# Last layer norm of a graph transformer block: which engine finishes which tile, and who issues the stores

## The chip, the core and the metric

The kernel runs on one core of a Trainium2 chip. The core has five engines with queues of their own: TensorE (PE, matrix products), VectorE (DVE), ScalarE (ACT), GpSimd (POOL) and SyncE (SP, which here only issues transfers). They wait for one another by semaphores. SBUF is the on-chip memory with 128 partitions; PSUM holds the results of TensorE in eight banks of 128 x 512 fp32. The metric is the device time of one execution in microseconds; the median of several runs counts.

## What is computed

The reference takes 1250 nodes with 512 features each and 41,250 edges. It normalizes `x`, sends it through a two-layer graph network and a linear attention, adds both to `x`, and then adds a feed-forward block whose weights are mixed from eight experts by a gate. Only the last lines matter here:

```python
h = jax.nn.relu(jnp.einsum('bsd,bfd->bsf', x, W1m) + b1m[:, None, :])
out = jnp.einsum('bsf,bdf->bsd', h, W2m) + b2m[:, None, :]
res = x + out
mu = res.mean(axis=-1, keepdims=True)
var = res.var(axis=-1, keepdims=True)
return (res - mu) * jax.lax.rsqrt(var + LN_EPS) * lng + lnb
...
x = x + _L0_ffn_ref(_layernorm(x, axis=-1)[None], ...)[0]
```

For each row: the second product (256 to 512), plus the normalized input, a mean and a variance over 512 columns, the difference scaled by `lng`, plus `lnb`, plus the row of `x`.

## The kernel before, in words

The 1250 rows are ten tiles of 128 rows (`NT` = 10, the last has 98). The whole kernel is one straight program of some 7,000 instructions: input norm, the adjacency matrix counted from the edge list, two graph layers as dense products with it, the attention, the middle norm, the gate, and the feed-forward block. From line 1200 on, the order of the work is written out by hand (`given()`, a manual schedule): each engine takes its instructions in the order in which the program names them, and a wait holds up all that is queued behind it on that engine.

The change touches the last stage. Before it, the merged weights `m1` and `m2` are done, `joined` (line 1325) has made the hidden layer `a_t`, and `xn2` (the normalized input) has had the second bias added, tiles 0 to 4 by VectorE and tiles 5 to 9 by GpSimd (lines 1364 and 1366). `x_sb` holds the row of `x` with `lnb` added already, `ln_g` holds the scale.

For a tile `t` the last stage has these steps:

- `out_product` (line 1374): TensorE makes the second product in a fresh PSUM bank; ten tiles use eight banks in turn.
- `out_sum` (line 1378): VectorE adds `xn2` in place, in PSUM.
- `out_gauge`: `spread` (lines 586 to 590) has VectorE take `bn_stats` and `bn_aggr` (mean and variance in `mv`) and ScalarE the square root of variance plus epsilon (`rs`).
- then one of two ways to finish. `out_far` (tiles 0, 1, 3, 4, 6, 7, 8): ScalarE negates the mean (1402), VectorE takes the reciprocal (1403), ScalarE multiplies the two (1404) and normalizes the tile from PSUM to a row buffer in SBUF (`normal`, line 600), and GpSimd multiplies by `ln_g` (1406) and adds `x_sb` (1407). `out_near` (tiles 2, 5, 9): VectorE does it alone with two `scalar_tensor_tensor` instructions and a reciprocal between them (1392 to 1394).
- a store of 256 KB to `out`, issued by SyncE; tile 9's (98 rows, 196 KB) by ScalarE.

The loop at line 1410 sets the order: at step `t`, the product and sum of tile `t`, then the finish of tile `t - 1`, then the statistics of tile `t`. On VectorE, then, the finish of a near tile stands between the sum and the statistics of the next tile. The row buffers come from two groups: even tiles take one of three (`row`), odd tiles one of four (`xt`), so tiles 6, 8 and 9 wait until the stores of tiles 0, 2 and 1 have landed. `small` gives four buffers each for `mv` and `rs`.

After the last step each engine loads one flag (line 1419) and branches over a general version of the kernel that these inputs don't need (line 1426).

Of the kernel before, what the change touches and what calls it, by code (L numbers as in the profile page):

```python
# [9 lines left out]
F32 = mybir.dt.float32  # L10
# [3 lines left out]
AF = mybir.ActivationFunctionType  # L14
ALU = mybir.AluOpType
AX = mybir.AxisListType

P = 128
N = 1250
D = 512  # L20
DT = D // P
NT = 10
# [22 lines left out]
def rows(t):  # L45
    return min(P, N - t * P)
# [479 lines left out]
def usual_block(  # L526
# [23 lines left out]
    nc = tc.nc  # L550
# [4 lines left out]
    small = ctx.enter_context(tc.tile_pool(name="small", bufs=4))  # L555
# [9 lines left out]
    def large(place, shape, dtype=F32, name="large"):  # L565

        return big.tile(shape, dtype, tag=place, name=name)
# [12 lines left out]
    eps = const.tile([P, 1], F32, name="eps")  # L580
    nc.vector.memset(eps, EPS)

    def spread(src, n):

        st = small.tile([P, 6], F32, name="st")
        nc.vector.bn_stats(st[:n], src)  # L586
        mv = small.tile([P, 2], F32, name="mv")
        nc.vector.bn_aggr(mv[:n], st[:n])
        rs = small.tile([P, 2], F32, name="rs")
        nc.scalar.activation(rs[:n, 0:1], mv[:n, 1:2], AF.Sqrt, bias=eps[:n])  # L590
        return mv, rs
# [7 lines left out]
    def normal(dst, src, rs, n):  # L599
        nc.scalar.activation(dst, src, AF.Identity, bias=rs[:n, 1:2], scale=rs[:n, 0:1])  # L600
# [85 lines left out]
    for t in range(NT):  # L686
        n = rows(t)
# [453 lines left out]
    ln_g = late.tile([P, D], F32, name="ln_g")  # L1141
# [29 lines left out]
    xn2 = large("A", [P, NT, D], name="xn2")  # L1171
# [92 lines left out]
    for t in range(NT):  # L1264
        n = rows(t)
# [95 lines left out]
    for t in range(NT):  # L1361
        n = rows(t)
# [5 lines left out]
    last = {}  # L1368

    def out_product(t):  # L1370
        n = rows(t)
        last[t] = bank()
        for f in range(FT):
            nc.tensor.matmul(last[t][:n], a_t[:, f, t * P:t * P + n], m2[:, f, :], start=(f == 0), stop=(f == FT - 1))  # L1374

    def out_sum(t):
        n = rows(t)
        nc.vector.tensor_tensor(last[t][:n], last[t][:n], xn2[0:n, t, :], ALU.add)

    def out_gauge(t):  # L1380
        last[t] = (last[t],) + spread(last[t][:rows(t)], rows(t))

    def out_row(t):
        tag, bufs = (("row", 3), ("xt", 4))[t % 2]
        return tmp.tile([P, D], F32, tag=tag, bufs=bufs, name="m")

    def out_near(t):

        n = rows(t)
        ps, mv, rs = last[t]  # L1390
        m = out_row(t)
        nc.vector.scalar_tensor_tensor(ps[:n], ps[:n], mv[:n, 0:1], ln_g[:n], op0=ALU.subtract, op1=ALU.mult)
        nc.vector.reciprocal(rs[:n, 0:1], rs[:n, 0:1])
        nc.vector.scalar_tensor_tensor(m[:n], ps[:n], rs[:n, 0:1], x_sb[0:n, t, :], op0=ALU.mult, op1=ALU.add)
        (nc.scalar if t == NT - 1 else nc.sync).dma_start(out=out[t * P:t * P + n, :], in_=m[:n])

    def out_far(t):

        n = rows(t)
        ps, mv, rs = last[t]  # L1400
        m = out_row(t)
        nc.scalar.mul(mv[:n, 0:1], mv[:n, 0:1], -1.0)
        nc.vector.reciprocal(rs[:n, 0:1], rs[:n, 0:1])
        nc.scalar.activation(rs[:n, 1:2], mv[:n, 0:1], AF.Copy, scale=rs[:n, 0:1])
        normal(m[:n], ps[:n], rs, n)
        nc.gpsimd.tensor_tensor(m[:n], m[:n], ln_g[:n], ALU.mult)  # L1406
        nc.gpsimd.tensor_tensor(m[:n], m[:n], x_sb[0:n, t, :], ALU.add)  # L1407
        nc.sync.dma_start(out=out[t * P:t * P + n, :], in_=m[:n])

    for t in range(NT + 1):  # L1410
        if t < NT:
            out_product(t)
            out_sum(t)
        if t >= 1:
            (out_near if t - 1 in (2, 5, 9) else out_far)(t - 1)
        if t < NT:
            out_gauge(t)
    last_order.close()
# [4 lines left out]
def graph_block(tc, *args):  # L1423

    unusual = usual_block(tc, *args)
    with tc.If(unusual > 0):
        general_block(tc, *args)
# [58 lines left out]
```

## Time and profile before

| | |
|---|---|
| three runs | 574.11, 574.61, 574.74 us, median 574.61 |
| the profiled execution | 574.88 us |
| its span, first to last instruction | 572.9 us |
| mean granted TensorE clock | 0.981 |
| busy: PE, DVE, ACT, POOL | 546.3, 324.8, 242.0, 80.1 us |
| last stage: first and last product | 541.42, 558.75 us |
| last compute instruction of VectorE | 563.15 to 563.90 us |
| last compute instruction of GpSimd | 565.97 to 567.23 us |
| last store issued by SyncE | 567.26 us |

The profile is of one execution. Positions such as 541.42 are microseconds from the first instruction. A row in the lists of groups gives the line, the engine, the instruction, what it writes and reads, how often it ran, its busy time in all and the mean length of one in nanoseconds. PE busy is not PE at its peak, since matmuls are pipelined. L600, L586, L588 and L590 are lines of helpers that several stages use. In the last stage alone, by the list of groups from 541 us on, one of each took:

| line | engine | what | ns |
|---|---|---|---|
| 1378 | DVE | sum, 128 x 512 in PSUM | 688 |
| 586 | DVE | statistics | 695 |
| 588 | DVE | aggregate | 182 |
| 1403 | DVE | reciprocal, one column | 157 |
| 600 | ACT | normalize, PSUM to SBUF | 777 |
| 590 | ACT | square root, one column | 286 |
| 1402 | ACT | negation, one column | 188 |
| 1404 | ACT | product, one column | 294 |

### The profile page before, as it was taken

How to read it: one execution, taken by the hardware profiler on the slowest of the kernel's cores; microseconds unless marked ns; L12 is line 12 of the kernel's file. 1: busy time of each engine (PE TensorE's matmuls, PEld its weight loads, DVE VectorE, ACT ScalarE, POOL GpSimd, SP SyncE). 2: the span in 40 equal slices, each digit the busy share in tenths (PEclk: the TensorE clock that was granted, in tenths of full speed). 3: DMA queues.
4: the chain of work that ended last, by engine and by line, in shares of the span. 5: the costliest groups of instructions: out<-in, count | busy, mean ns of one | idle time of the engine just before them, and what ended most of it. 6: DMA issues, size and time to landing. Idle time of an engine off the chain costs nothing.

```text
span 572.9 us, 6957 instructions
## 1 busy us (share of the span) xinstructions
PE 546.3 (95%) x2367; PEld 369.1 (64%) x2367; DVE 324.8 (57%) x1097; ACT 242.0 (42%) x533; POOL 80.1 (14%) x77
## 2 busy tenths in 40 slices
PE   8799999999999999999999999999999999997990
PEld 7665568799955477777854454459995557764540
DVE  4579999976899734444425534111113248708693
ACT  5676664454444112322333443113323456727242
POOL 7200000000000000000013331000000001106975
PEclk9899999999999999999999999999999999997995
DMA  9400200020030020000311002000009120402023
GB/s 287 176 1 1 74 2 1 1 74 2 1 113 36 0 74 0 1 1 1 111 37 52 22 1 73 0 0 1 2 0 348 55 74 1 146 1 75 0 76 110
DMA packets 19285, 29.10 MB, mean 51 GB/s; under 512 B 1529, under 2 KB 8185, under 8 KB 19240
## 3 DMA queue, kind: packets, MB, share of 16 engines
q1 hardware_dynamic: 18984, 28.32, 14.6%
q8 instruction: 20, 0.33, 0.2%
q10 hardware_dynamic: 256, 0.25, 0.2%
q14 instruction: 25, 0.20, 0.1%
HBM read 26.01 MB, written 2.56 MB: 50 GB/s over the span
## 4 chain that ended last, share of the span: by engine, by line
PE 87%; DVE 5%; ACT 3%; POOL 2%; issue 1%; DMA 1%; POOLq 0%; DVEq 0%; ACTq 0%
PE bank L576 28%; PE bank L981 16%; PE bank L968 12%; PE bank L917 6%; PE bank L1037 6%; PE bank L849 5%; PE bank L1064 5%; PE bank L1325 3%; PE bank L606 2%; PE bank L1374 1%; POOL m L1406 1%; POOL m L1407 1%; DVE st L586 1%; PE bank L902 1%; ACT xn L600 1%
## 5 line engine op out<-in xcount | busy, mean ns | idle before, releaser
L981 PE MATMUL bank<-adj,y_h 128*128 128x416 f32 (+1 forms) x240 | 86.5, 361 | 1.1 <-DVE adj L851 1.1
L981 PE MATMUL bank<-adj,y_l 128*128 128x416 f32 (+1 forms) x240 | 84.4, 352 | 0.0
L834 DVE TENSOR_SCALAR oh_k<-count,e_d 128x240 f16<-128x240 f16 x324 | 82.6, 274 | 0.0
L1083 POOL TENSOR_TENSOR m<-m,ls_bc 128x512 f32<-128x512 f32 (+1 forms) x10 | 12.7, 1269 | 447.3 <-ACT m L600 447.3
L968 PE MATMUL bank<-w,h_t 128*128 128x512 f32 (+1 forms) x160 | 70.4, 592 | 0.0
L576 PE MATMUL bank<-z_t,w 128*128 128x416 f32 (+1 forms) x192 | 68.9, 513 | 0.0
L576 PEld LDWEIGHTS bank<-z_t,w 128*128 128x128 f32 x192 | 36.1, 189 | 31.8 <-issue 29.9
L832 DVE TENSOR_SCALAR oh_s<-count,s_lo 128x128 f16<-128x128 f16 x220 | 54.1, 246 | 0.0
L968 PEld LDWEIGHTS bank<-w,h_t 128*128 128x128 f32 (+1 forms) x160 | 29.4, 188 | 34.8 <-issue 34.5
L614 DVE SCALAR_TENSOR_TENSOR z_t<-u,m_sb,z_t 128x416 f32<-128x416 f32 (+1 forms) x24 | 15.7, 653 | 59.8 <-ACT u L613 59.8
L981 PEld LDWEIGHTS bank<-adj,y_h 128*128 128x128 f32 x240 | 45.1, 188 | 2.6 <-issue 2.1
L981 PEld LDWEIGHTS bank<-adj,y_l 128*128 128x128 f32 x240 | 45.2, 188 | 1.2 <-issue 0.7
L849 PE MATMUL bank<-oh_k,oh_s 128*128 128x240 f16 x324 | 41.4, 266 | 1.4 <-ACT oh_s L818 1.2
L849 PEld LDWEIGHTS <-oh_s 128*128 128x128 f16 x324 | 31.6, 98 | 15.8 <-issue 5.1
L612 ACT ACTIVATE z_t<-bank,v_sb 128x416 f32<-128x416 f32 (+1 forms) x24 | 14.6, 608 | 61.5 <-PE bank L981 61.5
L851 DVE TENSOR_TENSOR adj<-adj,bank 128x240 f32 x81 | 32.3, 399 | 13.9 <-PE bank L849 12.5
L995 DVE BATCH_NORM_STATS2 bst<-bank 128x6 f32<-128x416 f32 (+1 forms) x24 | 14.4, 600 | 42.9 <-ACT h_t L994 42.9
L917 PE MATMUL bank<-kk,xn 128*128 128x128 f32 (+1 forms) x320 | 38.4, 275 | 0.0
L576 PE MATMUL bank<-xn_t,lw 128*128 128x256 f32 (+2 forms) x128 | 37.6, 439 | 0.3 <-ACT xn_t L607 0.3
L917 PEld LDWEIGHTS bank<-kk,xn 128*128 128x128 f32 (+1 forms) x320 | 37.0, 192 | 0.1
L1064 PE MATMUL bank<-mixer,q_t 128*128 128x512 f32 (+1 forms) x80 | 36.3, 592 | 0.0
L576 PE MATMUL bank<-xn_t,gw 128*128 128x256 f32 (+2 forms) x128 | 35.3, 427 | 0.9 <-ACT xn_t L607 0.9
(166 smaller groups left out, 800.0 us busy)
## 6 DMA issues: line engine op xcount, KB each, us to landing
t<-in_tv_w SPq DMA_DIRECT2D x12, 512.0 KB, 7.5
w<-in_conv_w SPq DMA_DIRECT2D x4, 1024.0 KB, 5.5
x_in<-in_x SPq DMA_DIRECT2D x9, 256.0 KB, 4.6
xt<-in_x SPq DMA_DIRECT2D x9, 256.0 KB, 4.1
out<-m SPq DMA_DIRECT2D x9, 256.0 KB, 2.4
rest<-in_tv_w SPq DMA_DIRECT2D x4, 512.0 KB, 4.8
lw<-in_lin_w SPq DMA_DIRECT2D x4, 256.0 KB, 4.9
wk<-in_w_qkv SPq DMA_DIRECT2D x1, 1024.0 KB, 7.0
```

What stands on the lines that cost most here:

```text
L576: nc.tensor.matmul(ps[:, :cn], lhs(c), rhs(c), start=(c == 0), stop=(c == k - 1))
L614: nc.vector.scalar_tensor_tensor(dst, u[:, :cn], minus(*slope), dst, op0=ALU.mult, op1=ALU.add)
L832: nc.vector.tensor_scalar(oh_s[:, j, :], count16[:, 0:P], s_lo[:, b, j:j + 1], None, op0=ALU.is_equal)
L834: nc.vector.tensor_scalar(oh_k[:, j, :], count16, key[:, b, j:j + 1], None, op0=ALU.is_equal)
L849: nc.tensor.matmul(ps[:, 0:NT * W], oh_s[:, j, :], oh_k[:, j, :], start=(j == 0), stop=(j == J - 1))
L851: nc.vector.tensor_tensor(adj_r[:, :, at], adj[:, :, at], ps[:, 0:NT * W].rearrange("p (s d) -> p s d", s=NT), ALU.add)
L917: nc.tensor.matmul(ps[:, c * P:(c + 1) * P], xn[0:n, t, c * P:(c + 1) * P], k_nodes(f)[0:n, t, :], start=(t == 0), stop=(t == NT - 1))
L968: nc.tensor.matmul(ps[:n], h_t[:, c, t * P:t * P + n], w1[:, c, :], start=(c == 0), stop=(c == DT - 1))
L981: nc.tensor.matmul(ps[:, :cn], y[0:n, s, f * P:(f + 1) * P], adj_r[0:n, s, c0:c0 + cn], start=(s == 0 and y is ys[0]), stop=(s == NT - 1 a ...
L1037: nc.tensor.matmul(ps[:n], xn_t[:, c, t * P:t * P + n], wq[:, c, :], start=(c == 0), stop=(c == DT - 1))
L1064: nc.tensor.matmul(ps[:n], q_t[:, h, t * P:t * P + n], mixer[:, h, :], start=(h == 0), stop=(h == DT - 1))
L1325: nc.tensor.matmul(ps[:, :cn], m1[:, c, f * P:(f + 1) * P], xn2_t[:, c, c0:c0 + cn], start=(c == 0), stop=(c == DT - 1))
```

## The change

Tiles 4, 5, 7, 8 and 9 are finished by VectorE (`NEAR`), tiles 0, 1, 2, 3 and 6 by ScalarE and GpSimd. For four of the near tiles, 5, 7, 8 and 9 (`BY_SCALAR`), the sum also gives the row's total (`accum_out`), and ScalarE makes the statistics: the negated mean, the square of each difference summed over the row (the squares themselves go to the row buffer and are written over later), and the square root. VectorE adds this negated mean where it subtracted the mean. These four tiles are finished three steps after their sum, at the head of a step, ahead of that step's sum; tile 4 is finished one step after its sum, also at the head. All ten stores are issued by SyncE.

```diff
+    NEAR, BY_SCALAR = (4, 5, 7, 8, 9), (5, 7, 8, 9)
+
     def out_sum(t):
         n = rows(t)
-        nc.vector.tensor_tensor(last[t][:n], last[t][:n], xn2[0:n, t, :], ALU.add)
+        ps = last[t]
+        if t in BY_SCALAR:
+            mv = small.tile([P, 2], F32, name="mv")
+            nc.vector.scalar_tensor_tensor(ps[:n], ps[:n], 1.0, xn2[0:n, t, :], op0=ALU.mult, op1=ALU.add,
+                                           accum_out=mv[:n, 0:1])
+            last[t] = ps, mv
+        else:
+            nc.vector.tensor_tensor(ps[:n], ps[:n], xn2[0:n, t, :], ALU.add)
 
     def out_gauge(t):
-        last[t] = (last[t],) + spread(last[t][:rows(t)], rows(t))
+        n = rows(t)
+        if t in BY_SCALAR:
+            ps, mv = last[t]
+            rs = small.tile([P, 2], F32, name="rs")
+            m = out_row(t)
+            nc.scalar.mul(mv[:n, 0:1], mv[:n, 0:1], -1.0 / D)
+            nc.scalar.activation(m[:n], ps[:n], AF.Square, bias=mv[:n, 0:1], accum_out=mv[:n, 1:2])
+            nc.scalar.activation(rs[:n, 0:1], mv[:n, 1:2], AF.Sqrt, bias=eps[:n], scale=1.0 / D)
+            last[t] = ps, mv, rs, m
+        else:
+            last[t] = (last[t],) + spread(last[t][:n], n) + (None,)
...
     def out_near(t):
         n = rows(t)
-        ps, mv, rs = last[t]
-        m = out_row(t)
-        nc.vector.scalar_tensor_tensor(ps[:n], ps[:n], mv[:n, 0:1], ln_g[:n], op0=ALU.subtract, op1=ALU.mult)
+        ps, mv, rs, m = last[t]
+        m = out_row(t) if m is None else m
+        nc.vector.scalar_tensor_tensor(ps[:n], ps[:n], mv[:n, 0:1], ln_g[:n],
+                                       op0=ALU.add if t in BY_SCALAR else ALU.subtract, op1=ALU.mult)
         nc.vector.reciprocal(rs[:n, 0:1], rs[:n, 0:1])
         nc.vector.scalar_tensor_tensor(m[:n], ps[:n], rs[:n, 0:1], x_sb[0:n, t, :], op0=ALU.mult, op1=ALU.add)
-        (nc.scalar if t == NT - 1 else nc.sync).dma_start(out=out[t * P:t * P + n, :], in_=m[:n])
+        nc.sync.dma_start(out=out[t * P:t * P + n, :], in_=m[:n])
...
-    for t in range(NT + 1):
+    for t in range(NT + 3):
+        for u in NEAR:
+            if u == t - (3 if u in BY_SCALAR else 1):
+                out_near(u)
         if t < NT:
             out_product(t)
             out_sum(t)
-        if t >= 1:
-            (out_near if t - 1 in (2, 5, 9) else out_far)(t - 1)
+        if 0 < t <= NT and t - 1 not in NEAR:
+            out_far(t - 1)
         if t < NT:
             out_gauge(t)
```

In the built program VectorE's order from tile 4 on is: sum 4, reciprocal 3, statistics and aggregate 4, finish 4, sum 5, sum 6, statistics and aggregate 6, sum 7, reciprocal 6, finish 5, sum 8, sum 9, finish 7, finish 8, finish 9. In the new file the far way's GpSimd passes are lines 1428 and 1429, the near finish lines 1413 to 1416, the accumulating sum line 1384, the plain sum line 1388, ScalarE's statistics lines 1397 to 1399, the stores lines 1417 and 1430, the flag line 1444.

More of the change, by code (lines that the diff above doesn't have):

```diff
@@ L1389, in out_near @@
         n = rows(t)
-        ps, mv, rs = last[t]
-        m = out_row(t)
-        nc.vector.scalar_tensor_tensor(ps[:n], ps[:n], mv[:n, 0:1], ln_g[:n], op0=ALU.subtract, op1=ALU.mult)
+        ps, mv, rs, m = last[t]
+        m = out_row(t) if m is None else m
+        nc.vector.scalar_tensor_tensor(ps[:n], ps[:n], mv[:n, 0:1], ln_g[:n],
+                                       op0=ALU.add if t in BY_SCALAR else ALU.subtract, op1=ALU.mult)
         nc.vector.reciprocal(rs[:n, 0:1], rs[:n, 0:1])
         nc.vector.scalar_tensor_tensor(m[:n], ps[:n], rs[:n, 0:1], x_sb[0:n, t, :], op0=ALU.mult, op1=ALU.add)
-        (nc.scalar if t == NT - 1 else nc.sync).dma_start(out=out[t * P:t * P + n, :], in_=m[:n])
+        nc.sync.dma_start(out=out[t * P:t * P + n, :], in_=m[:n])
     def out_far(t):
         n = rows(t)
-        ps, mv, rs = last[t]
+        ps, mv, rs, _ = last[t]
         m = out_row(t)
```

## The prediction

> **What bounds the kernel now.** I read the granted clock first (0.981 for the whole span), then the chain that ended last in its last 50 us, then busy time by stretch for the end, then the engines' timelines there. The profiled execution took 574.88 us for a span of 572.9. TensorE carries the chain until tile 2 of the last product. The chain's view of the final stretch (start, length, what) then ends on GpSimd:
>
> ```profile
> 541.59 6.88 PE bank L1374 x16
> ...
> 558.66 0.79 ACT m L600
> 559.52 1.27 POOL m L1406
> 560.86 1.26 POOL m L1407
> ...
> 566.43 0.80 POOL m L1407
> ```
>
> Two stretches of the view of busy time (length; then PE, PEld, DVE, ACT, POOL busy with counts; clock, DMA share, GB/s) show what runs while GpSimd finishes:
>
> ```profile
> 560.00:567.30 7.30, 0.00 (x0) 0.00 (x0) 3.70 (x9) 2.51 (x7) 7.00 (x6) 0.59 0.41 148
> 567.30:573.00 5.70, 0.00 (x0) 0.00 (x0) 0.00 (x0) 0.00 (x0) 0.00 (x0) 0.50 0.15 53
> ```
>
> TensorE is done at 558.75. GpSimd works 7.00 of the next 7.30 us, VectorE 3.70. Seven of ten tiles go through GpSimd at two passes of 1.264 us (rows of lines 1406 and 1407), 2.55 us a tile, while VectorE needs 1.55 us for its share of such a tile. The last store, tile 8's, is issued by SyncE at 567.26, when GpSimd stops. From there to the end of the span are 5.68 us without a compute instruction. In SyncE's own waits,
>
> ```profile
> SPq L1426 <- SPq L1426: 2.7, 1, 2.7
> ```
>
> is its branch after the last store: code that it waits for, not data. The store's data landed 2.06 us after its issue and is covered. So the end stands 5.68 us behind SyncE's last store, and the question is when that is issued after the change.
>
> **The units of the sum.** From the timeline (start, length, engine, line, instruction), VectorE only, then the end of tile 9:
>
> ```profile
> 554.52 0.68 DVE L1378 TENSOR_TENSOR bank<-bank,xn 128x512 f32<-128x512 f32 x1
> 555.11 0.75 DVE L1392 SCALAR_TENSOR_TENSOR bank<-bank,mv,ln_g 128x512 f32<-128x512 f32 x1
> 555.77 0.15 DVE L1393 RECIPROCAL rs<-rs 128x1 f32<-128x1 f32 x1
> 555.96 0.75 DVE L1394 SCALAR_TENSOR_TENSOR m<-bank,rs,x_sb 128x512 f32<-128x512 f32 x1
> 556.62 0.69 DVE L586 BATCH_NORM_STATS2 st<-bank 128x6 f32<-128x512 f32 x1
> 557.35 0.18 DVE L588 BATCH_NORM_AGGREGATE mv<-st 128x2 f32<-128x6 f32 x1
> 557.45 0.68 DVE L1378 TENSOR_TENSOR bank<-bank,xn 128x512 f32<-128x512 f32 x1
> 558.04 0.15 DVE L1403 RECIPROCAL rs<-rs 128x1 f32<-128x1 f32 x1
> 558.16 0.70 DVE L586 BATCH_NORM_STATS2 st<-bank 128x6 f32<-128x512 f32 x1
> ...
> 563.15 0.75 DVE L1394 SCALAR_TENSOR_TENSOR m<-bank,rs,x_sb 98x512 f32<-98x512 f32 x1
> 563.94 0.60 ACTq L1395 DMA_DIRECT2D out<-m  x1
> ```
>
> Neighbours overlap, so I count from start to start: sum to the next 0.59 (0.71 where statistics follow a sum at once); reciprocal to statistics 0.12; statistics to aggregate 0.73 to 0.74; aggregate to the next sum 0.10, but 0.21 where the next one needs its result (562.03 to 562.24 in tile 9). A near finish is 0.66 + 0.19 + 0.66 = 1.51. A store follows its finish by 0.04 (563.90 to 563.94).
>
> **Part 1, GpSimd loses tiles 4, 7 and 8, and keeps 0, 1, 2, 3 and 6.** Six passes go, 6 x 1.264 = 7.6 us. It starts at 547.16 as before. Its tile 3 is done four tiles of 2.58 us later, at 557.5. Tile 6 waits for ScalarE's normalization, at about 558.0 by the count below, so GpSimd stops near 560.6. It leaves the path; VectorE is late next.
>
> **Part 2, VectorE.** It gains two near finishes (five for three), drops four statistics and four aggregates, and its sum in tiles 5, 7, 8 and 9 becomes a scalar_tensor_tensor with an accumulated row sum. The trace has no such instruction. Without the accumulator its row is that of line 1392: 0.75 us, 0.66 to the next. For the accumulator I call the extra r. Here the Trainium skill speaks against the change: "VectorE: DVE Perf Modes", section "Two Vector instructions with no wait between them", says that an operation that also writes out its accumulator is two instructions, the main one and an accumulator read. The trace has it on ScalarE alone:
>
> ```profile
> L1198 ACT ACTIVATION_READ_ACCUMULATOR u<-bank,v_sb 128x1 f32 x16 | 3.1, 193 | 0.0
> ```
>
> I take r = 0.19 from this row, near VectorE's own one-column rows (0.15 reciprocal, 0.18 aggregate). Without a second instruction r is 0. At most I allow 0.35, the read plus the 0.09 of overlap and about 0.07 of start lost.
>
> Up to the sum of tile 3 at 548.49 nothing differs. Sums 0 to 3 stand at TensorE's pace, (548.49 - 543.34) / 3 = 1.72, so sum 4 starts at 550.21. Then, in the built program's order:
> - to sum 5: 0.59 (reciprocal 3), 0.12, 0.74, 0.21, and the near finish of tile 4, 1.51: 553.38.
> - to sum 6: 0.66 + r = 0.85: 554.23.
> - to sum 7: 0.71 + 0.73 + 0.10: 555.77.
> - to sum 8: 0.85, 0.12, near finish of tile 5, 1.51: 558.25.
> - to sum 9: 0.85: 559.10. TensorE has it ready at 550.21 + 5 x 1.72 = 558.81.
> - near finishes of 7, 8 and 9: first at 559.95, then 561.46 and 562.97. Tile 9's last instruction starts at 563.82 and ends at 564.57.
>
> The last store is issued at 564.61: **2.65 us before 567.26**. With r = 0 VectorE runs into TensorE at sum 9, and the gain is 3.1. With r = 0.35 it is 2.0.
>
> **Part 3, ScalarE.** Each scalar tile has a negation (0.19), the Square with its accumulator (0.78 by line 600's row, then a 0.19 read that overlaps it by 0.09), and a square root (0.28), with small gaps 1.33 us. Reciprocal 6, at 556.62, lets it normalize tile 6 at 557.21. Tiles 7, 8 and 9 follow: Squares read out at about 559.0, 560.3 and 561.7, where VectorE asks at 559.95, 561.46 and 562.97. Cover: 1.0 to 1.3 us. Beyond it, each us that ScalarE is late counts in full.
>
> A second rule speaks against this part: "ScalarE: Activation LUTs", section "What ACT_TABLE_LOAD costs", puts every switch to a different table set at about 2.66 us. The trace agrees: 1.283 for the row, 2.70 from the load at 66.90 to the next activation. If Square and Sqrt were in different sets, four tiles would make up to eight switches, over 21 us. The built program has a load at the same three places as before, none among these lines; I take nothing.
>
> **Part 4, stores.** Order on SyncE: tiles 0, 1, 2, 3, 4, 6, 5, 7, 8, 9. Tile 4 waits behind tile 3 (557.5) and tile 5 behind tile 6 (560.6); nobody reads either row buffer again. The stores of 7, 8 and 9 come 1.51 us apart, and an issue takes 0.33 to 0.38, once 1.20, so SyncE keeps up. A load of 98 rows took it 0.36. ScalarE's 0.60 issue goes. Row buffers of tiles 6, 8 and 9 wait for stores 0, 2 and 1, landed by about 557.5. All this is nothing; if the last issue takes 1.20, it costs 0.85.
>
> **Sum.** 574.88 - 2.65 = 572.2 against the profiled execution, which is 0.27 above the median. Against the median, 574.61 - 2.65: **572.0 us**.
>
> **Rivals.**
> - *The cover is thinner* (12%): ScalarE's steps wait on one another and take half as long again, 2.0 us a tile for 1.33: tile 9's read comes at 563.7, 0.7 late; with 0.3 of a longer tail behind the last store 1.0 is lost: 573.0. For it: the engines' code fetches come closer together. Against: two stores were in flight at the earlier fetches too.
> - *The accumulating sum runs at half rate* (9%): 512 elements more at VectorE's pace (the step from 256 to 512 elements, 0.489 to 0.756, gives 0.53), four times that is 2.1 us: gain about 0.5, 574.1, no change. Against: without an accumulator it runs at one pace from PSUM and SBUF (416 columns from SBUF took 0.653, on the line between those two). VectorE's turn-over is at r = 0.85.
> - *Square and Sqrt evict each other's table* (6%, with any other cause of slower): six switches after tile 6's normalization, 16.2 us, less 1.3 of cover, on top of 572.0: about 587. It turns slower from 4 us of ScalarE delay over three tiles (1.3 + 2.65). Against it stands the built program.
>
> **Numbers.** Forecast 73%, rivals 12, 9 and 6. About 0.2% (1.15 us) can be told from no change: faster 0.85, same 0.09, slower 0.06. The forecast's own range is 3.1 to 2.0 of gain with 0.3 of scatter: 571.2 to 572.9. Reaching over the first rival: 571.2 to 573.5.
>
> **What would show it.** Right: the chain ends on VectorE, line 1416 of the new kernel; TensorE's end unmoved; GpSimd idle after 560.6; SyncE's last issue near 564.6 with about 5.7 us behind it; an accumulator-read row of about 0.19 on VectorE. Wrong: a gap on VectorE before line 1413 put down to ScalarE (cover too thin), a long row for line 1384 (half rate), a table load among lines 1397 to 1399, or SyncE's last issue late though VectorE was not.

## The result and the profile after

The changed kernel takes **571.18 us** (median of six runs, 570.89 to 572.49), the kernel before beside it 574.39 (six runs, 573.93 to 575.25). The ratio is 0.9948, with a 95% interval from 0.9936 to 0.9959, or 2.4 to 3.7 us less. A second set of five runs gave 571.63 us and 0.9947 (0.9932 to 0.9961).

The profiled execution took 570.89 us, its span is 569.1 us, the mean granted clock 0.989. The span is 3.86 us shorter than before's, but 1.02 us of that lies ahead of the edit: the last product starts at 540.40 instead of 541.42. The second profile of the same changed kernel, at a clock of 0.984, starts it at 541.48. That microsecond comes and goes with the clock: over the thirteen profiles of this document the last product starts at 540.1 to 540.8 us where the clock was 0.986 or more, and at 541.3 to 541.6 us where it was 0.985 or less. So below I count from the start of the first last product: before, 25.84 us to SyncE's last store and 5.68 from there to the end of the span, 31.52 in all; after, 22.80 and 5.88, 28.68 in all. The gain is 2.8 us, made of 3.04 in the stage less 0.2 in the tail.

The chain that ended last, its last pieces (start, length, what), now lies on VectorE:

```profile
561.57 0.75 DVE bank L1413
562.32 0.07 DVE rs L1415
562.39 0.02 issue
562.42 0.75 DVE m L1416
```

Busy time for the two stretches from TensorE's end on, in the columns of the earlier view:

```profile
557.70:563.20 5.50, 0.03 (x1) 0.00 (x0) 5.14 (x11) 2.49 (x9) 1.53 (x2) 0.99 0.70 260
563.20:569.10 5.90, 0.00 (x0) 0.00 (x0) 0.00 (x0) 0.00 (x0) 0.00 (x0) 0.50 0.15 46
```

GpSimd is busy 1.53 us of this stretch, where it had 7.00 of 7.30. VectorE fills 5.14 of 5.50: it is the one that finishes. Behind it stands the same empty tail. SyncE's waits still name the branch:

```profile
SPq L1451 <- SPq L1451: 2.5, 1, 2.5
```

During that wait, from 564.7 to 567.1 us, the view of the DMA queues has three packets on an instruction queue (packets, MB, share of the DMA engines):

```profile
q14 instruction: 3, 0.02, 3.2%
```

That SyncE waits for code is read from these two lines. VectorE's own branch falls into the same stretch, so not every packet need be SyncE's.

VectorE's timeline (start, length, engine, line, instruction, with the idle time ahead of it in brackets) shows both the new instruction and what limits the end:

```profile
552.39 0.69 DVE L1384 SCALAR_TENSOR_TENSOR bank<-bank,xn 128x512 f32<-128x512 f32 x1
553.00 0.14 DVE L1384 DVE_READ_ACCUMULATOR bank<-bank,xn 128x1 f32 x1
553.00 0.73 DVE L1388 TENSOR_TENSOR bank<-bank,xn 128x512 f32<-128x512 f32 x1
...
557.38 0.14 DVE L1384 DVE_READ_ACCUMULATOR bank<-bank,xn 128x1 f32 x1
557.87 0.70 DVE L1384 SCALAR_TENSOR_TENSOR bank<-bank,xn 98x512 f32<-98x512 f32 x1 [0.34 <-ACT rs L1399]
558.48 0.14 DVE L1384 DVE_READ_ACCUMULATOR bank<-bank,xn 98x1 f32 x1
558.48 0.76 DVE L1413 SCALAR_TENSOR_TENSOR bank<-bank,mv,ln_g 128x512 f32<-128x512 f32 x1
```

The accumulator read is an instruction of its own, 0.14 us long, but the sum of tile 6 starts in the same hundredth of a microsecond, 0.61 after the accumulating sum. Ahead of sum 9 VectorE is idle. The view names ScalarE, whose square root in tile 7 ended at 557.86. But sum 9 does not read it, and TensorE ended its last product at 557.73, 0.14 before sum 9; the first sum, at 542.31, follows the first tenth of the products (540.40 and 1.73) by 0.18. So I read it as a wait for TensorE. From sum 8 to sum 9 it is 1.09 us from start to start, where the accumulating sums before took 0.61 to the next instruction.

ScalarE's statistics, in the list of groups from the last stage on (busy us, mean ns of one, idle ahead):

```profile
L1398 ACT ACTIVATE m<-bank,mv 128x512 f32<-128x512 f32 x3 | 2.1, 689 | 0.1
...
L1398 ACT ACTIVATION_READ_ACCUMULATOR m<-bank,mv 128x1 f32 x3 | 0.6, 193 | 0.0
```

The Square is shorter than line 600's normalization (777), and its read of 193 is the row that the prediction had borrowed. The statistics are ready when VectorE asks for them. For tile 9, the last one, from both engines' timelines:

```profile
559.85 0.19 ACT L1398 ACTIVATION_READ_ACCUMULATOR m<-bank,mv 98x1 f32 x1
...
561.57 0.75 DVE L1413 SCALAR_TENSOR_TENSOR bank<-bank,mv,ln_g 98x512 f32<-98x512 f32 x1
```

### The profile page after: what moved, and what is told of

It reads as the page before. It is cut to its first block, busy times and chain, and to the rows that moved or that the text cites. A ratio compares the mean times of both kernels' runs of the same rounds, so it can differ in the third digit from the quotient of the medians.

```text
span 569.1 us, 6958 instructions
## 1 busy us (share of the span) xinstructions
PE 545.6 (96%) x2367; PEld 368.1 (65%) x2367; DVE 324.7 (57%) x1097; ACT 244.2 (43%) x539; POOL 75.3 (13%) x73
## 5 line engine op out<-in xcount | busy, mean ns | idle before, releaser
L834 DVE TENSOR_SCALAR oh_k<-count,e_d 128x240 f16<-128x240 f16 x324 | 84.4, 281 | 0.0
L832 DVE TENSOR_SCALAR oh_s<-count,s_lo 128x128 f16<-128x128 f16 x220 | 55.8, 254 | 0.0
```

Source lines behind the costliest of these rows:

```text
L832: nc.vector.tensor_scalar(oh_s[:, j, :], count16[:, 0:P], s_lo[:, b, j:j + 1], None, op0=ALU.is_equal)
L834: nc.vector.tensor_scalar(oh_k[:, j, :], count16, key[:, b, j:j + 1], None, op0=ALU.is_equal)
```

## The experiments

The table has them all, counted from the first of the last products in each profile: to the last store of any engine, and to the end of the span. Times are medians, ratios are to the kernel before.

| kernel | last store | span's end | us | ratio (95%) |
|---|---|---|---|---|
| before | 25.84 | 31.52 | 574.4 | |
| changed | 22.80 | 28.68 | 571.18 | 0.9948 (0.9936 to 0.9959) |
| changed, again | 22.80 | 28.81 | 571.63 | 0.9947 (0.9932 to 0.9961) |
| statistics by VectorE | 26.50 | 32.84 | 575.44 | 1.0016 (1.0009 to 1.0023) |
| before, one store queue | 26.27 | 32.62 | 575.68 | 1.0022 (1.0014 to 1.0029) |
| finish after one step | 28.30 | 34.49 | 577.64 | 1.0056 (1.0042 to 1.007) |
| finish after two steps | 23.98 | 29.93 | 573.20 | 0.998 (0.997 to 0.999) |
| ten more accumulators | 22.91 | 28.65 | 571.09 | 0.9942 (0.9928 to 0.9956) |
| flag early | 22.80 | 27.99 | 571.18 | 0.9949 (0.9936 to 0.9963) |
| tile 7 one step sooner | 22.48 | 28.84 | 571.11 | 0.9947 (0.9933 to 0.9961) |
| last store by ScalarE | 22.81 | 27.88 | 570.56 | 0.9931 (0.9915 to 0.9946) |
| tile 7 sooner, flag early | 22.48 | 27.58 | 570.14 | 0.9929 (0.9915 to 0.9942) |
| all three | 22.48 | 26.84 | 569.31 | 0.9913 (0.9898 to 0.9929) |

**The changed kernel again.** No edit.

> The changed kernel once more, as the measure for the parts. Theory (GpSimd leaves the path, VectorE and then TensorE's last product set the end): 571.0 to 571.6 us, last store issued 22.8 us after the first of the last products, where the kernel before needs 25.8. Rival (the earlier start of the last stage, 540.4 against 541.4, is part of the change): the last stage starts about 1 us earlier than before's in this run too. Theory: its start follows the granted clock alone and can lie either way.

571.63 us. The last store comes 22.80 us after the first product, as in the first profile, while the product itself starts 1.08 us later than there. The earlier start was no part of the change.

**The division of the tiles alone.** VectorE keeps its five finishes and makes their statistics too:

```diff
-    NEAR, BY_SCALAR = (4, 5, 7, 8, 9), (5, 7, 8, 9)
+    NEAR, BY_SCALAR = (4, 5, 7, 8, 9), ()
```

> Only the division of the tiles and the one store queue: tiles 4, 5, 7, 8 and 9 are finished by VectorE, but with its own statistics, one step after their sum. Theory (VectorE is filled by the five finishes, so ScalarE's statistics carry the gain): VectorE ends about 26.2 us after the first of the last products, later than GpSimd did before: 574.4 to 575.2 us, no gain. Rival (relief of GpSimd alone is the gain): 571 to 572 us.

575.44 us, 0.16% slower than before and 0.2 above the expected range. All five finishes now stand one step behind their sum. GpSimd is done 21.42 us after the first product, and that gains nothing: VectorE needs 3.2 us for each near tile with its own statistics, as between the finishes of tiles 4 and 5, and ends at 26.47 with tile 9:

```profile
550.55 0.76 DVE L1413 SCALAR_TENSOR_TENSOR bank<-bank,mv,ln_g 128x512 f32<-128x512 f32 x1
...
553.75 0.76 DVE L1413 SCALAR_TENSOR_TENSOR bank<-bank,mv,ln_g 128x512 f32<-128x512 f32 x1
...
565.81 0.75 DVE L1416 SCALAR_TENSOR_TENSOR m<-bank,rs,x_sb 98x512 f32<-98x512 f32 x1
```

This run has the single store queue too, and the next one shows that the queue alone costs as much; set against that one, the division by itself comes out even, not slower. The gain belongs to the pair, GpSimd relieved and VectorE's statistics given to ScalarE. The other half of the pair, ScalarE's statistics with GpSimd keeping its seven tiles, was not run. That it gains nothing is argued from the profile before: there GpSimd was the last to finish, 3.3 us behind VectorE.

**The store queue alone**, on the kernel before:

```diff
-        (nc.scalar if t == NT - 1 else nc.sync).dma_start(out=out[t * P:t * P + n, :], in_=m[:n])
+        nc.sync.dma_start(out=out[t * P:t * P + n, :], in_=m[:n])
```

> The kernel before with tile 9's store issued by SyncE, as the only edit. Theory: in SyncE's queue it stands behind tile 8's store, which waits for GpSimd until 567.3, so the last issue moves back by one issue, 0.4 us: 574.6 to 575.0 us, none of the gain. Rival (one queue shortens the end, by ScalarE's 0.6 us issue and its later branch): 573.6 to 574.2 us.

575.68 us: a loss, above the expected range, and larger than the 0.43 us by which the last store moved back. SyncE's tail is 6.36 us instead of 5.68: its last issue took 0.65 us where it had taken 0.33, and its flag load 0.93 us where it had taken 0.51.

**The lag of three steps**, cut to one and to two:

```diff
-            if u == t - (3 if u in BY_SCALAR else 1):
+            if u == t - 1:
```

```diff
-            if u == t - (3 if u in BY_SCALAR else 1):
+            if u == t - (2 if u in BY_SCALAR else 1):
```

> The changed kernel with tiles 5, 7, 8 and 9 finished one step after their sum, not three. Theory (from a sum to the finish of its tile ScalarE needs 1.85 us, and each is now uncovered): VectorE waits in each of the four tiles, tile 7 longer because ScalarE has tile 6's normalization ahead of it; the last finish comes about 5 us later than in the changed kernel: 575.5 to 577 us, slower than before. Rival (the lag is idle, ScalarE is quick enough): 571 to 572 us.

> The changed kernel with tiles 5, 7, 8 and 9 finished two steps after their sum. Theory (the third step covers ScalarE where it has tile 6's normalization ahead of tile 7's statistics): VectorE now finishes tile 5 before sum 7, so reciprocal 6 and with it ScalarE's tile 6 and 7 come 1.5 us later, tile 7's finish waits ahead of sum 9; last store 23.5 to 24.3 us after the first of the last products, against 22.80: 572.1 to 573.0 us. Rival (two steps are enough cover everywhere): 571.2 to 571.8 us, last store within 0.2 of 22.80.

577.64 and 573.20 us, 0.6 and 0.2 above the expected ranges. With one step VectorE waits for ScalarE's Square in all four tiles. From its timeline, the finishes of tiles 5 and 7:

```profile
555.10 0.76 DVE L1413 SCALAR_TENSOR_TENSOR bank<-bank,mv,ln_g 128x512 f32<-128x512 f32 x1 [1.08 <-ACT m L1398]
...
561.14 0.76 DVE L1413 SCALAR_TENSOR_TENSOR bank<-bank,mv,ln_g 128x512 f32<-128x512 f32 x1 [2.19 <-ACT m L1398]
```

The four waits are 1.08, 2.19, 1.13 and 1.08 us, 5.5 in all, and the last store is 5.5 us later than in the changed kernel. With two steps one wait is left, ahead of tile 7's finish:

```profile
558.97 0.76 DVE L1413 SCALAR_TENSOR_TENSOR bank<-bank,mv,ln_g 128x512 f32<-128x512 f32 x1 [1.54 <-ACT m L1398]
```

That is where ScalarE has tile 6's normalization ahead of it, as expected.

**What an accumulator costs.** One more on each large instruction of the five finishes:

```diff
+    spare = small.tile([P, 2 * NT], F32, name="spare")
...
-                                       op0=ALU.add if t in BY_SCALAR else ALU.subtract, op1=ALU.mult)
+                                       op0=ALU.add if t in BY_SCALAR else ALU.subtract, op1=ALU.mult,
+                                       accum_out=spare[:n, 2 * t:2 * t + 1])
...
-        nc.vector.scalar_tensor_tensor(m[:n], ps[:n], rs[:n, 0:1], x_sb[0:n, t, :], op0=ALU.mult, op1=ALU.add)
+        nc.vector.scalar_tensor_tensor(m[:n], ps[:n], rs[:n, 0:1], x_sb[0:n, t, :], op0=ALU.mult, op1=ALU.add,
+                                       accum_out=spare[:n, 2 * t + 1:2 * t + 2])
```

> The changed kernel with an accumulator output, read by nobody, added to both large instructions of all five finishes on VectorE: ten more, six of them behind sum 9 where nothing covers them. Theory from the trace (VectorE's accumulator read of 0.14 us lies beside the next instruction): at most 0.2 us over the changed kernel, 571.2 to 571.8 us. Rival (an accumulator read costs the 0.19 us that the prediction gave it): 1.1 us more behind sum 9, 572.3 to 572.9 us, last store 23.9 us after the first of the last products.

571.09 us. Two rows of its list of groups (busy us, mean ns of one):

```profile
L1414 DVE DVE_READ_ACCUMULATOR bank<-bank,mv,ln_g 128x1 f32 x4 | 0.6, 143 | 0.0
...
L1418 DVE DVE_READ_ACCUMULATOR m<-bank,rs,x_sb 128x1 f32 x4 | 0.3, 83 | 0.0
```

The reads are there, and the last store moved from 22.80 to 22.91 us, with six of them behind sum 9: 0.02 us each.

**The tail.** Every engine loads the flag ahead of the last stage's loop:

```diff
+    flag = nc.values_load(unusual, min_val=0, max_val=1,
+                          skip_runtime_bounds_check_because="it is the result of comparisons")
     for t in range(NT + 3):
...
-    return nc.values_load(unusual, min_val=0, max_val=1,
-                          skip_runtime_bounds_check_because="it is the result of comparisons")
+    return flag
```

> The changed kernel with the flag loaded by every engine before the last stage, not after it; the branch stays at the end. Theory (behind SyncE's last store stand, one after another, the flag load of 0.96 to 1.03 us, the branch and a code fetch of 2.5 us): the load leaves the path, 0.9 to 1.1 us less than the changed kernel: 570.2 to 570.8 us. Rival (the end waits for the store's data or for the other engines' code, and the load lies beside that): 571.2 to 571.8 us.

The two views disagree here. The profile has the tail at 5.18 us instead of 5.88 and 6.01, so the load did stand on the path. SyncE's records divide the tail into four stretches, each counted from start to start: last store to flag load, load to branch, branch to SyncE's next instruction, and from there to the end (us):

| kernel | store | load | branch | rest | tail |
|---|---|---|---|---|---|
| before | 0.38 | 0.58 | 2.76 | 1.96 | 5.68 |
| before, one store queue | 0.70 | 1.00 | 2.70 | 1.96 | 6.36 |
| changed | 0.40 | 1.03 | 2.50 | 1.96 | 5.88 |
| changed, again | 0.40 | 1.10 | 2.55 | 1.96 | 6.01 |
| flag early | 0.44 | none | 2.77 | 1.97 | 5.18 |
| tile 7 one step sooner (below) | 0.40 | 1.17 | 2.83 | 1.96 | 6.36 |

The rest is the same in all. Without the load a stretch of 1.03 to 1.10 us is gone, but the one behind the branch is 0.2 to 0.3 longer, so 0.7 to 0.8 is left. The length of the load itself, before the change and after it (ns least, median, most; start), stands in the views of its line:

```profile
L1419 SPq TENSOR_LOAD <-unusual x1: 514/514/514, 567.6 to 567.6; - x1
...
L1444 SPq TENSOR_LOAD <-unusual x1: 962/962/962, 563.6 to 563.6; - x1
```

The median, 571.18 us, misses the expected 570.2 to 570.8: it shows nothing of this gain against the first set of the changed kernel and 0.45 against the second. Three of its five runs had a granted clock of 0.984, where runs of the changed kernel at 0.983 to 0.984 took 571.81 to 572.49; these took 571.18 to 571.65. By itself the time doesn't settle it. The combinations below do better: with tile 7 sooner, 571.11 us without the early flag and 570.14 with it.

**Tile 7 one step sooner**, ahead of sum 9, where VectorE had been idle:

```diff
-            if u == t - (3 if u in BY_SCALAR else 1):
+            if u == t - {4: 1, 5: 3, 7: 2, 8: 3, 9: 3}[u]:
```

> The changed kernel with tile 7 alone finished two steps after its sum, so ahead of sum 9, where VectorE has about 0.5 us without work until TensorE is done. Theory (the end is sum 9 plus the finishes that stand behind it): sum 9 comes later by 1.0 to 1.3 us, but one finish of 1.5 us fewer stands behind it; the last store 22.4 to 22.6 us after the first of the last products, against 22.80: 0.2 to 0.4 us less than the changed kernel. Rival (sum 9's own delay decides, since ScalarE's statistics of tile 9 start later and are uncovered): 22.9 or later, no gain or a loss.

The last store comes 0.32 us sooner, as expected, but the time stayed at 571.11 us, level with the changed kernel's 571.18. The tail of this profile is 6.36 us, and so what the last store gained was given back: the load is 0.1 longer than in the changed kernel and the stretch behind the branch 0.3. Whether the edit made them longer or they vary by themselves, one profile does not show.

**One part of the change undone**: tile 9's store by ScalarE, in the changed kernel.

```diff
-        nc.sync.dma_start(out=out[t * P:t * P + n, :], in_=m[:n])
+        (nc.scalar if t == NT - 1 else nc.sync).dma_start(out=out[t * P:t * P + n, :], in_=m[:n])
```

> The changed kernel with one part undone: tile 9's store is issued by ScalarE again. Theory (behind the last issue stand that engine's own flag load, branch and code fetch, and SyncE has nine semaphore waits after its own): SyncE is done with tile 8's store 1.5 us earlier and runs its code fetch and waits beside ScalarE's; ScalarE issues at 22.8 and has 0.6 + 0.9 + 2.6 us ahead of it: 0.5 to 1.0 us less than the changed kernel, 570.2 to 570.9 us. Rival (one queue is at least as good, or SyncE's waits for the last store's landing take its place): 571.2 us or more.

570.56 us, and 27.88 us to the end of the span instead of 28.68 and 28.81. SyncE branches 2.0 us earlier in the stage; in its waits stands what sets the end now, ScalarE's branch:

```profile
SPq L1507 <- ACTq L1451: 0.5, 1, 0.5
```

Part of the rival holds too: SyncE also waited about 0.6 us for the last store to land before that. The intervals of this ratio and the changed kernel's overlap, so the time alone leaves it likely; the profile and the same edit on the kernel before point the same way.

**Together.** Tile 7 sooner and the flag early, then tile 9's store by ScalarE as well:

> Tile 7 finished two steps after its sum, and the flag loaded ahead of the last stage. Theory (the first moves the last store from 22.80 to 22.48, the second takes 0.7 to 1.0 us out of the tail, and the two add up): last store at 22.5, 5.2 us of tail: 1.0 us less than the changed kernel, 570.1 to 570.7 us. Rival (they fall on the same slack): 570.8 to 571.4 us.

> The same, and tile 9's store by ScalarE. Theory: ScalarE issues at 22.5, then branch and fetch, 0.6 + 2.7 us, then the final barrier of 1 us; SyncE is ready by then: 1.5 to 2.2 us less than the changed kernel, 569.1 to 569.9 us. Rival (SyncE's waits, or the store's landing 2.0 to 2.7 us after its issue, set the end): 570.1 us or more.

570.14 and 569.31 us. All three together beat the changed kernel clear of the noise (0.9913, at most 0.9929, against 0.9948, at least 0.9936) and the kernel before by 5.1 us.

## Why the prediction was right, point by point

The forecast was 572.0 us, from a gain of 2.65; measured were 571.18 and 571.63, gains of 3.2 and 2.75 against the kernel before beside them. The way was right. The first set lies level with the low edge of the range, 571.2, partly because of the clock: its four runs at 0.989 or more took 570.89 to 571.22 us, its two at 0.983 took 571.86 and 572.49. In the profile the gain is 2.8, and that it comes so near to 2.65 is in part luck: the stage gained 0.39 more than worked out, and the tail, put down as unchanged, gave 0.2 back (0.3 in the second profile).

- *The end stands a fixed stretch behind SyncE's last store.* Right in kind: 2.5 us behind the branch, read as a code fetch, and no compute. Not fixed: 5.88 and 6.01 us instead of 5.68. The flag load, which the working did not name, took 0.96 to 1.03 us instead of 0.51, and the stretch behind the branch, 0.2 to 0.3 shorter, hid about half of that. The load was long in every profile in which SyncE's last store was tile 9's and the load came after it (0.80 to 1.10), and 0.51 where tile 8's was last. Why, no run shows.
- *GpSimd leaves the path.* Right. It stops 18.91 us after the first product; the working had 19.2.
- *VectorE's sum.* The steps held, but the term r was mis-sized, and with it the plain price of the instruction. It had 0.66 + 0.19 from an accumulating sum to the next instruction; measured 0.61, in four tiles 0.96 too much. The read exists, as the Trainium skill has it ("VectorE: DVE Perf Modes", section "Two Vector instructions with no wait between them"), 0.14 us long, but beside the next instruction. The sum itself took 0.69 instead of 0.75: its scalar is a constant, where line 1392's is a column. TensorE took half of the 0.96 back, since sum 9 had to wait for it and came 1.09 instead of 0.61 after sum 8. With some 0.1 in other steps, the last store came at 22.80 us where the working has 23.19. This is the case r = 0 of the working, a gain of 3.1; the stage gained 3.04.
- *ScalarE is covered.* Right. VectorE asked for the statistics of tiles 7, 8 and 9 1.0, 1.2 and 1.5 us after they were read out. The working's four pieces add up to 1.35 us a tile, not 1.33; measured were 1.24 and 1.28 from tile to tile. One-step and two-step lags show that the cover is real work: 5.5 and 1.2 us without it. The Square was cheaper than the row that I took, 0.689 instead of 0.777: line 600 has a column each for scale and bias, the Square for the bias alone. The Trainium skill, "ScalarE: Activation LUTs", section "What ACT_TABLE_LOAD costs", puts each such column at about 93 ns; the two rows differ by 88.
- *No table load.* Right: three loads of 1.283 us in the whole program, as before. But the trace was misread as agreeing with the 2.66 us of a switch. The 2.70 from the load at 66.90 to the next activation are not the load's: that activation waited for VectorE's `k_m`, which ended at 69.57 (lines below). No run here shows what a switch costs beyond the 1.283, so the rival's 16.2 us rest on the figure that the prediction cites.
- *Stores cost nothing.* Wrong by size. The order and waits came as worked out, but the single queue costs: 1.1 us behind the first product on the kernel before, 0.8 to 0.9 on the changed one. The working counted ScalarE's 0.60 as saved, and did not ask what each engine has behind its own last store.
- *The rivals.* None came. Half rate fell with 0.69 us a sum, table loads with their count. The thinner cover did not come, though its longer tail did, by 0.2 to 0.3 us.

The lines on the table load, from the profile before (start, length, engine, line, instruction):

```profile
66.90 1.28 ACT L890 ACT_TABLE_LOAD   x1
...
69.43 0.14 DVE L887 TENSOR_REDUCE k_m<-k_m 128x1 f32<-128x3 f32 x1
...
69.60 0.61 ACT L890 ACTIVATE kk<-bank,k_m 128x418 f32<-128x418 f32 x1 [1.42 <-DVE k_m L887]
```

## What to carry to other kernels

When a slow helper engine is relieved, count what the relief puts on the engine that takes over: here it gained nothing until a third engine took the statistics, and that only with finishes put late enough to cover its chain. Read the end of the program engine by engine, down to what each does after its last store: two edits there, the flag load and the last store's queue, took 0.7 to 0.9 us each out of the profiled stage and tail, beside the change's 2.8. Price a new instruction by its own operands and start to start, not by a longer neighbour and a whole extra read.

## What the runs showed that I had not expected

- VectorE's accumulator read takes 0.08 to 0.14 us in the trace and delays the next instruction by 0.02 us; ten more of them moved the last store by 0.11.
- A column as scalar costs VectorE's scalar_tensor_tensor 0.06 us over 512 columns: lines 1413 and 1416, with a column, both take 0.751, though one writes to PSUM and the other to SBUF. Line 1384 has the two operations of line 1416 and a constant, and takes 0.689.
- With four stores close together, the changed kernel's last store landed 3.15 us after its issue in the first profile (563.20 to 566.35) and 2.70 in the second, where before's last took 2.06. SyncE looked for it 1.2 us or more after that, so it cost nothing here.
